# A causal attention block on one core: queries and keys projected for one unit at a time, fixed steps for each kind of piece, and a refilled opening and closing

## The chip, the cores and the metric

The kernel runs on one core of a Trainium2 chip. A core has five engines that work side by side, each with its own queue of instructions: TensorE (PE in the profile; its weight loads are listed apart as PEld), VectorE (DVE), ScalarE (ACT), GpSimd (POOL), and SyncE (SP), which in this kernel issues nearly all transfers (DMAs). Engines wait for one another through semaphores. The metric is the device time of one execution in microseconds (us); lower is better. All numbers are float32.

## The reference

The input x has 8 batches of 1024 tokens of 256 numbers. The block is a sandwich: half a routed feed-forward, attention, half a routed feed-forward, each added to x.

```python
x = x + 0.5 * ffn(layernorm(x), gate_w, w1, b1, w2, b2)
x = x + attention(layernorm(x), Wq, bq, Wkv, bkv, Wo, bo)
x = x + 0.5 * ffn(layernorm(x), gate_w, w1, b1, w2, b2)

# attention: 16 heads of 16 numbers, causal
dots = einsum('bhid,bhjd->bhij', q * scale, k)
attn = softmax(where(j > i, -1e9, dots))
out  = einsum('bhij,bhjd->bhid', attn, v) @ Wo.T + bo

# ffn: softmax gate over 8 experts, the two best of each token
counts = bincount(a_e, length=8)
keep   = counts <= cap            # an expert with more than cap tokens is dropped whole
```

With 8192 tokens, two experts each and 8 experts, cap is 1280 while the mean count is 2048, so an expert is kept only if it is chosen far less than the mean.

## The kernel before

**Two parts, of which one runs.** The kernel computes attention on x at once and, beside it, counts for both feed-forwards how many tokens choose each expert (`choose` L334, `tally`, `fewest` L397). Only if some expert has at most cap tokens does a branch (L1309) run the feed-forward and, where needed, the attention again. With these inputs no branch is taken, so the time is that of one call of `attention` (L681). The gate of the first feed-forward comes out of extra columns of the value projection, that of the second out of extra columns of the output projection; that is why both are 256 + 8 = 264 wide.

**Units and steps.** A unit u is four heads g of one batch b (u = 4b + g), 32 units in all, and one more, u = -1, in which only the first half of the work below exists for unit 0. Each unit has 24 steps. In a step PE computes two kinds of score blocks, each as matmuls on 32 by 64 tiles of the array: `sc` for the exponentials of unit u (`e_steps` L911: ACT exponentiates the block into `pT`, POOL masks a diagonal block by a select, PE later multiplies `pT` by the values into `pav`), and `sm` for the row maxima of unit u+1 (`m_steps` L865: DVE takes a maximum over each block; `settle` L899 sends the maxima by DMA into a row of `qT`, so that the next pass subtracts them inside its matmul). The widths of a step's blocks follow the causal mask: 512 in steps 0 and 1, 384 in 2 and 3, 256 in 4 and 5, 128 in 6 and 7, 512 in 8 to 17, 384 in 18 and 19, 256 in 20 and 21, 128 in 22 and 23. There are six score buffers of one PSUM bank each, taken in turn (`score` L695), and two banks for everything else (`bank` L699). Attention values of a step are issued two and three steps after its scores; steps 0, 2, 8 and 10 have none.

**Pieces beside the steps.** All other PE work is cut into pieces and put one (or half of one) into a step. `pq` is a projection of 512 tokens to queries or keys (eight matmuls of 512, in two half-steps); ACT adds the bias, and eight DMAs carry each head of 16 rows to its place in `qT` or `kT`. `pv` is the values of 128 tokens, `px` the output projection of 128 tokens (both eight matmuls of 264, in two half-steps), `pta` four transposes of the normalised input. Class `Beside` (L52) hands them out: each work is a Python generator that yields PIECE (wants to begin a piece), REST (the second half, at the next step) or a number of steps to wait. `Beside.step(begin)` lets the first work in its list that asks for a PIECE have one, if `begin` is true. Steps 4 to 7 and 20 to 23, where DVE has most to do for each step, begin none unless two works ask at once (L1288).

**What runs beside which unit.** `prepare` (L727) loads the next batch and takes its statistics on DVE; `enter` (L750) normalises on POOL, four tiles ahead (`bufs=4`, L759), and transposes in g = 1; `values_of` (L776) follows in g = 2 and 3; `residual` (L807) adds the output bias to x on POOL; `project` (L825) stands in g = 0 and in g = 2, each time for two units (u+2 and u+3): weights of keys and of queries are kept apart (`wkT`, `wqT`), a column group of 128 holds eight heads of one kind, and there are four pieces (keys and queries for each half of the tokens), three steps apart. `leave` (L987) reads the attention of one half of a batch back from DRAM, takes reciprocals of the row sums, multiplies (two POOL multiplications, L1012, two steps apart), and then gives four px pieces; it begins at step 9 of g = 3 for the first half and at step 2 of the next batch's g = 0 for the second. `gate_first` (L817) and `regate` (L1114) are the chains of small DVE operations of the gates. Statistics of the output rows are put in `light` (L1029), and one is taken per step.

**Order.** `InOrder` (L27) chains every instruction of PE, DVE, ACT and POOL in the order in which the Python code issues it, so a waiting instruction holds all behind it on its engine. Since this helper records them, nearly every line of the profile says L37; groups are told apart by the names of their tiles. SP's DMAs go in program order too.

**Opening and closing.** Before unit -1 the first batch is normalised and `project(0, ...)` makes keys and queries for units 0 and 1, half by half (L1174 to L1182); the DMAs of the second unit's heads go out behind each half (L861). In unit -1 run the turning of the value weights and the first half of the values (L1186), and in unit 0 the rest of the weights' work (`turning`: wos, then `gcs`, `pt_gc`, `pg`, `pb_v`, L255 to L290), the other values, `gate_first(0)` and the projection for units 2 and 3. In the last unit no maxima are left; `divided`, `leave_first` and `leave_last` (L1038 to L1111) take the attention of the last four heads straight from PSUM, transposing it (`pt_last`), dividing, transposing back (`on_last`) and projecting (`px_last`). After the last step what is left in `beside` is finished (L1292), then the first gate's count (L1294), then the second half's `leave_last` and `regate`.

Of the kernel before, what the change touches and what calls it, by code (L numbers as in the profile page):

```python
# [10 lines left out]
F32 = mybir.dt.float32  # L11
# [37 lines left out]
PIECE, REST = "piece", "rest"  # L49


class Beside:  # L52
# [10 lines left out]
    def advance(self, work):  # L63
        ask = next(work[0], None)
        if ask is None:
            self.works.remove(work)
        else:
            work[1] = ask if ask in (PIECE, REST) else self.now + ask
        self.open = work if ask == REST else None if self.open is work else self.open

    def due(self):
        for work in list(self.works):
            while work in self.works and work[1] not in (PIECE, REST) and work[1] <= self.now:
                self.advance(work)
# [4 lines left out]
    def step(self, begin):  # L79
# [4 lines left out]
        elif begin:  # L84
            for work in self.works:
                if work[1] == PIECE:
                    self.advance(work)
                    break
# [12 lines left out]
def macaron_kernel(  # L101
# [98 lines left out]
    wqT = const.tile([P, DC, D], F32, name="wqT")  # L200
    wkT = const.tile([P, DC, D], F32, name="wkT")
# [5 lines left out]
    bqT = const.tile([P, DC], F32, name="bqT")  # L207
    bkT = const.tile([P, DC], F32, name="bkT")
# [6 lines left out]
    def weights(pool, bank, matmul, transpose):  # L215
# [6 lines left out]
        with nc.allow_non_contiguous_dma(reason="two vectors of 256"):  # L222
            for src, dst in ((bkv[:D], bkT), (bq, bqT)):
                nc.scalar.dma_start(out=dst, in_=src.rearrange("(c p) -> p c", p=P))
# [6 lines left out]
        with nc.allow_non_contiguous_dma(reason="two vectors of 256"):  # L231
            nc.sync.dma_start(out=boT, in_=bo.rearrange("(c p) -> p c", p=P))
            nc.sync.dma_start(out=bvT, in_=bkv[D:].rearrange("(c p) -> p c", p=P))

        gpsimd.tensor_scalar(bqT, bqT, QSCALE, None, ALU.mult)

        def turn(wsb, dst):
# [4 lines left out]
            scalar.copy(dst, pt.rearrange("p (c d) -> p c d", c=DC))  # L242

        turn(wks, wkT)
        yield PIECE
        turn(wqs, wqT)
# [9 lines left out]
        yield PIECE  # L256
# [4 lines left out]
        vector.tensor_scalar(gcs, gsb, mean, None, ALU.subtract)  # L261
        pt = bank("pt_gc")
# [4 lines left out]
        bo_cols = const.tile([P, DC, P], F32, name="bo_cols")  # L267
        gpsimd.tensor_copy(bo_cols, boT.unsqueeze(2).to_broadcast([P, DC, P]))
        bv_cols = const.tile([P, DC, P], F32, name="bv_cols")
        gpsimd.tensor_copy(bv_cols, bvT.unsqueeze(2).to_broadcast([P, DC, P]))  # L270
# [363 lines left out]
    def feed_forward(layer, logits, src, dst):  # L634
        stack = ExitStack()
        with stack:
# [15 lines left out]
            for b in range(B):  # L652
# [5 lines left out]
                for j in range(TB):  # L658
                    xn = norm.tile([P, D], F32, tag="xn", name=f"xn_n{layer}_{b}_{j}", bufs=4)
# [21 lines left out]
    def attention(run_no, src, dst, gate0, logits, tally):  # L681
# [3 lines left out]
        with stack:  # L685
# [64 lines left out]
            def enter(b):  # L750
# [3 lines left out]
                xns = {}  # L754

                def normed(jj):
                    xns[jj] = []
                    for j in (2 * jj, 2 * jj + 1):
                        xn = norm.tile([P, D], F32, tag="xn", name=f"xn_a{b}_{j}", bufs=4)  # L759
                        gpsimd.tensor_scalar(  # L760
                            xn, xb[:, j, :D], mv[:, j, 0:1], rstd[:, j : j + 1], ALU.subtract, ALU.mult
                        )
                        xns[jj].append(xn)

                normed(0)
                normed(1)
                yield 3
                for jj in range(TB // 2):
                    yield PIECE
                    turned(b, jj, xns.pop(jj))  # L770
                    if jj + 2 < TB // 2:
                        normed(jj + 2)
# [52 lines left out]
            def project(u, apart, parts=(0, 512)):  # L825
                b, g = divmod(u, NG)
                xnT = xnTs[b]
                gp = g // 2
                for s0 in parts:
                    others = []  # L830
                    for wT, bT, dsts, scale in ((wkT, bkT, kTs, 1.0), (wqT, bqT, qTs, QSCALE)):
                        yield PIECE
                        pq = bank(f"pq{u}_{s0}")
                        for c in range(DC):
                            matmul_cols(
                                pq,
                                wT[:, c, gp * P : (gp + 1) * P],
                                xnT[:, c, s0 : s0 + 512],
                                start=(c == 0),
                                stop=(c == DC - 1),  # L840
                            )
                            if c + 1 < DC:
                                yield REST
                        packed = ap.tile([P, 512], F32, tag="packed", name=f"packed{u}_{s0}", bufs=4)
                        scalar.activation(packed, pq, AF.Identity, bias=bT[:, gp : gp + 1], scale=scale)
                        for k in range(8):
                            r = 32 * (k % 4)
                            to = dsts[(u + k // 4) % 4][r : r + HD, s0 : s0 + 512]
                            head = packed[HD * k : HD * (k + 1), :]
                            if apart and dsts is qTs and k % 4 == 0 and u > 2:  # L850

                                nc.sync.dma_start(
                                    out=dsts[(u + k // 4) % 4][HD::32, s0 : s0 + 512], in_=zeros
                                )
                            if apart or k < 4:
# [503 lines left out]
```

## Time and profile before

| | us |
|---|---|
| median of three runs | 1393.98 (1392.86 to 1394.01) |
| the profiled execution | 1393.18 |
| its span, first to last instruction | 1391.50 |
| of it before unit -1 | 24.15 |
| unit -1 | 29.36 |
| unit 0 | 57.09 |
| units 1 to 30 | 1226.30 |
| unit 31 and the closing | 54.60 |

The profile is a hardware record of one execution. Its page gives the busy time of each engine, the chain of work that ended last, and groups of instructions with their mean durations in ns and the idle time of their engine just before them. Stretches of the span can be asked for by themselves, with the busy time and number of instructions of each engine; so can the instructions one by one, as a timeline with start, duration, engine, operation, the tile written and the tiles read, a repeat count, and in square brackets the idle time before and what ended it. The granted clock of TensorE is 0.983 over the span, 1.00 in units 1 to 30, 0.83 in unit -1, 0.85 in unit 0, and 0.81 in the last stretch. Over units 1 to 30 PE is busy for 1223.39 us, DVE for 942.70, ACT for 726.82 and POOL for 365.01.

### The profile page before, as it was taken

Reading aid. Unit: us, or ns where it says so; the run is one execution under the profiler, and the core shown is the slowest. Engines: PE = TensorE matmul, PEld = TensorE weight load, DVE = VectorE, ACT = ScalarE, POOL = GpSimd, SP = SyncE. Lnnn points to the kernel's source line nnn. Section 1 sums busy time; section 2 is a strip of 40 time slices with the busy share of each in tenths; the row PEclk is TensorE's granted clock in tenths of the full one; section 3 lists DMA queues with packets and bytes.
Section 4 is the critical chain, followed back from the end, with each engine's and each line's share of the span. In section 5 each row is a group of like instructions: output and inputs, shape, how many; then the busy total and the mean of one; then the engine's idle time right before and its main releaser. Section 6 shows DMA issues by size and latency. Waiting matters only on the chain.

```text
span 1391.5 us, 51072 instructions
## 1 busy us (share of the span) xinstructions
PE 1352.3 (97%) x20664; PEld 456.6 (33%) x20664; DVE 1029.7 (74%) x3417; ACT 788.0 (57%) x1790; POOL 399.0 (29%) x720
## 2 busy tenths in 40 slices
PE   6999999999999999999999999999999999999994
PEld 2333333333333333333333333333333333323331
DVE  4757677876878868777778777787687786778854
ACT  3246655565655656555655656555665565655561
POOL 3015114241143412352131421424114331222221
PEclk9889999999999999999999999999999999999997
DMA  4010111212112210212112121122112111122100
GB/s 149 10 41 27 42 27 50 60 60 77 35 56 61 73 47 30 79 51 72 41 36 71 45 88 34 48 66 73 53 33 60 57 47 44 44 66 65 43 27 33
DMA packets 67021, 73.70 MB, mean 53 GB/s; under 512 B 24688, under 2 KB 42232, under 8 KB 66776
## 3 DMA queue, kind: packets, MB, share of 16 engines
q1 hardware_dynamic: 65688, 69.82, 16.5%
q8 instruction: 164, 2.69, 0.8%
q14 instruction: 81, 0.66, 0.2%
q10 hardware_dynamic: 1088, 0.53, 0.1%
HBM read 26.87 MB, written 26.20 MB: 38 GB/s over the span
## 4 chain that ended last, share of the span: by engine, by line
PE 91%; DVE 4%; POOL 2%; issue 1%; SPq 1%; DMA 1%; ACT 0%; ACTq 0%; DVEq 0%; POOLq 0%
PE sc L37 40%; PE pav L37 23%; PE sm L37 9%; PE pq L37 8%; PE pv L37 4%; PE px L37 4%; PE pta L37 1%; DVE sm L37 1%; POOL rstd_a L37 1%; POOL xa L37 1%; DVE first L37 0%; DMA bqT<-in_L_attn_bq_dram 0%; SPq L862 0%; POOL pT L37 0%; SPq L856 0%
## 5 line engine op out<-in xcount | busy, mean ns | idle before, releaser
L37 ACT ACTIVATE pT<-sc 128x512 f32<-128x512 f32 (+3 forms) x1536 | 668.9, 489 | 515.2 <-PE sm L37 395.5
L37 PE MATMUL sm<-kT,qT 32*64 32x512 f32 (+3 forms) x6144 | 759.8, 511 | 1.5 <-DMA qT<-packed 0.4
L37 PE MATMUL sc<-qT,kT 32*64 32x512 f32 (+3 forms) x6144 | 709.2, 508 | 0.0
L37 POOL TENSOR_SCALAR_AFFINE_SELECT pT<-pT 128x256 f32<-128x256 f32 x512 | 208.1, 410 | 927.6 <-ACT pT L37 926.5
L37 DVE TENSOR_REDUCE first<-sm 128x1 f32<-128x512 f32 x512 | 328.2, 684 | 141.9 <-PE sm L37 136.2
L37 PE MATMUL pav<-pT,vaug 128*32 128x256 f32 (+2 forms) x5120 | 386.7, 370 | 3.9 <-POOL pT L37 3.9
L37 DVE CUSTOM_DVE_ANT_0 sm<-sm,causal,first 128x256 f32<-128x256 f32 (+3 forms) x512 | 261.2, 556 | 76.5 <-PE sm L37 67.2
L37 PEld LDWEIGHTS sc<-qT,kT 32*64 32x64 f32 x6144 | 188.5, 130 | 355.5 <-ACT pT L37 256.3
L37 DVE CUSTOM_DVE_ANT_0 sm<-sm,causal 128x256 f32<-128x256 f32 (+3 forms) x512 | 241.6, 515 | 79.0 <-PE sm L37 74.2
L37 PEld LDWEIGHTS pav<-pT,vaug 128*32 128x32 f32 x5120 | 104.0, 108 | 367.8 <-issue 289.6
L37 PEld LDWEIGHTS sm<-kT,qT 32*64 32x64 f32 x6144 | 213.9, 130 | 29.7 <-DVE top L37 14.4
L37 DVE DVE_READ_ACCUMULATOR2_ANT top<- 128x1 f32 x1024 | 145.0, 142 | 0.0
L37 PE MATMUL pv<-wvT,xnT 128*32 128x264 f32 x1024 | 83.7, 400 | 0.0
L37 PE MATMUL px<-woT,on 128*32 128x264 f32 x960 | 76.1, 389 | 0.0
L37 PE MATMUL pq<-xnT,wkT 128*32 128x512 f32 x512 | 68.0, 607 | 1.4 <-ACT xnT L37 1.4
L37 POOL TENSOR_SCALAR xn_a<-xa,mv_a,rstd_a 128x256 f32<-128x256 f32 x56 | 67.9, 1223 | 1.2 <-PE pta L37 1.0
L37 PE MATMUL pq<-xnT,wqT 128*32 128x512 f32 x512 | 66.8, 596 | 0.0
L37 POOL TENSOR_TENSOR on<-on,inv 128x512 f32<-128x512 f32 (+1 forms) x32 | 40.9, 1278 | 12.5 <-DMA inv<-inv_d 12.5
L37 PEld LDWEIGHTS pv<-wvT,xnT 128*32 128x32 f32 x1024 | 29.0, 111 | 43.6 <-issue 26.2
L37 POOL TENSOR_TENSOR xa<-xa,bo_all 128x528 f32<-128x528 f32 x32 | 42.0, 1311 | 0.6
L37 ACT COPY vaug<-pv 128x256 f32<-128x256 f32 x64 | 24.4, 381 | 26.6 <-PE pv L37 26.6
L37 PEld LDWEIGHTS px<-woT,on 128*32 128x32 f32 x960 | 27.9, 109 | 35.1 <-issue 11.4
(126 smaller groups left out, 482.2 us busy)
## 6 DMA issues: line engine op xcount, KB each, us to landing
att_d<-att SPq DMA_DIRECT2D x62, 256.0 KB
kT<-packed SPq DMA_DIRECT2D x256, 32.0 KB
qT<-packed SPq DMA_DIRECT2D x256, 32.0 KB
out_dram<-xa SPq DMA_DIRECT2D x16, 512.0 KB
on<-att_d SPq DMA_DIRECT2D x30, 256.0 KB
inv<-inv_d SPq DMA_DIRECT2D x30, 256.0 KB
xa<-in_L_attn_x_dram SPq DMA_DIRECT2D x7, 1024.0 KB
xa<-in_L_attn_x_dram SPq DMA_DIRECT2D x2, 512.0 KB
```

The costliest lines, as they stand in the source:

```text
L37: i = call(*args, **kwargs)
```

## The change

The weights of keys and queries are laid side by side in `wkqT`, the scale of the queries multiplied in when the weights are turned, so that one piece of 128 columns makes keys and queries of one unit (four heads each). `project(u)` has two pieces, one for each half of the tokens, and every unit but the last two runs one for unit u+2, as its first work. Its pieces are of a kind of their own (QK): they begin at step 0 or 8, and px, pv and pta pieces at the other steps. In `leave` the waits are shortened and the two multiplications follow one another, at the first step of a unit. `enter` normalises all eight tiles ahead (`bufs=8`) and its transposes follow. In the opening, `project(0)` is for unit 0 alone, `project(1)` is cut up into unit -1, which now takes two half-steps of pieces in each pair of steps, and `gcs` and the copies of the bias are computed three steps ahead of `pt_gc`. At the end, `leave_last` of the second half is interleaved with the rest of `regate` of the first half and with the first gate's count, and these with one another. The functions keep their arithmetic.

```diff
-PIECE, REST = "piece", "rest"
+PIECE, QK, REST = "piece", "qk", "rest"
...
-    def step(self, begin):
+    def step(self, kinds=()):
         self.now += 1
         self.due()
         if self.open is not None:
             self.advance(self.open)
-        elif begin:
+            return
+        for kind in kinds:
             for work in self.works:
-                if work[1] == PIECE:
+                if work[1] == kind:
                     self.advance(work)
-                    break
+                    return
...
-        turn(wks, wkT)
+        turn(wks, wkqT[:, :, :, 0, :], 1.0)
         yield PIECE
-        turn(wqs, wqT)
+        turn(wqs, wkqT[:, :, :, 1, :], QSCALE)
...
         turn(wos, woT[:, :, :D])
-        yield PIECE
...
         vector.tensor_scalar(gcs, gsb, mean, None, ALU.subtract)
+        bo_cols = const.tile([P, DC, P], F32, name="bo_cols")
+        gpsimd.tensor_copy(bo_cols, boT.unsqueeze(2).to_broadcast([P, DC, P]))
...
+        yield 2
+        yield PIECE
         pt = bank("pt_gc")
...
-                normed(0)
-                normed(1)
-                yield 3
+                for j in range(TB):
+                    xn = norm.tile([P, D], F32, tag="xn", name=f"xn_a{b}_{j}", bufs=8)
...
+                    if j % 2:
+                        yield 2
                 for jj in range(TB // 2):
                     yield PIECE
-                    turned(b, jj, xns.pop(jj))
-                    if jj + 2 < TB // 2:
-                        normed(jj + 2)
+                    turned(b, jj, xns[2 * jj : 2 * jj + 2])
...
-            def project(u, apart, parts=(0, 512)):
+            def project(u, parts=(0, 512)):
...
                 for s0 in parts:
-                    others = []
-                    for wT, bT, dsts, scale in ((wkT, bkT, kTs, 1.0), (wqT, bqT, qTs, QSCALE)):
-                        yield PIECE
...
+                    yield QK
+                    pq = bank(f"pq{u}_{s0}")
+                    for c in range(DC):
+                        matmul_cols(
+                            pq,
+                            wkqT[:, c, g].rearrange("p a d -> p (a d)"),
...
+                        if c + 1 < DC:
+                            yield REST
...
+                    for k in range(8):
+                        r = 32 * (k % 4)
+                        nc.sync.dma_start(
+                            out=(kTs, qTs)[k // 4][u % 4][r : r + HD, s0 : s0 + 512],
+                            in_=packed[HD * k : HD * (k + 1), :],
+                        )
...
             def leave(b, hf):
...
-                yield 2
+                waits = (2, 6, 5, 9) if hf else (2, 4, 4, 5)
+                yield waits[0]
...
-                yield 6
+                yield waits[1]
                 vector.reciprocal(sums, sums)
...
-                yield 4
+                yield waits[2]
...
-                yield 8
+                yield waits[3]
                 for c in range(DC):
                     gpsimd.tensor_tensor(on[:, c], on[:, c], inv[:, c], ALU.mult)
-                    yield 2
+                yield 2
...
-                drain(project(0, 0, (hf * 512,)))
+                drain(project(0, (hf * 512,)))
...
-            opening = beside.add(chain(some(turning, 2), values_of(0, 0, 0, HT)))
+            opening = beside.add(chain(some(turning, 2), project(1), values_of(0, 0, 0, HT)))
...
                 if u == 0:
                     beside.finish(opening)
+                    preparing = beside.add(prepare(1))
+                    opening = beside.add(values_of(0, 0, HT, TB), first=True)
+                    projecting = beside.add(project(2))
                     beside.add(chain((PIECE,), turning, residual(0), gate_first(0)))
...
+                    valuing = beside.add(values_of(b + 1, 0, 0, HT))
+                if u >= 0 and g == 3 and b + 1 < B:
+                    beside.finish(valuing)
+                    valuing = beside.add(chain(values_of(b + 1, 0, HT, TB), residual(b + 1)))
+                if u > 0:
+                    beside.finish(projecting)
+                    if u + 2 < NU:
+                        projecting = beside.add(project(u + 2), first=True)
...
-                    beside.step(True)
+                    for _ in range(2):
+                        beside.step((QK, PIECE))
...
-                    beside.step(k in long_steps or u == 0 or beside.pending() > 1)
+                    if u == 0:
+                        beside.step((PIECE, QK))
+                    elif k in (0, 8):
+                        beside.step((QK, PIECE))
+                    else:
+                        beside.step((PIECE,) if k in long_steps or beside.pending() > 1 else ())
...
-            while beside.works:
-                beside.finish(beside.works[0])
-            leasts = [None if gate0 is None else fewest("0", gate0[1], bank("cnt0"))]
-            drain(leave_last(B - 1, 1, last.pop(), (scalar.copy, vector.tensor_copy)))
+            while beside.open is not None or beside.pending():
+                beside.step((PIECE,))
+            leasts = [None]
+            for k, _ in enumerate(leave_last(B - 1, 1, last.pop(), (scalar.copy, vector.tensor_copy))):
+                for _ in range(3 if k < 2 else len(beside.works) * STEPS):
+                    beside.step()
+                if k == 1 and gate0 is not None:
+                    leasts = [fewest("0", gate0[1], bank("cnt0"))]
```

## The prediction, made before the changed kernel had run

> **What bounds the kernel now.** I read the page's busy shares and chain of waits first, then the busy time of each engine in chosen stretches, then the timeline of TensorE (PE) step by step, and last the built order of both kernels on each engine, which says in which step each instruction stands. The page:
>
> ```profile
> span 1391.5 us, 51072 instructions
> PE 1352.3 (97%) x20664; PEld 456.6 (33%) x20664; DVE 1029.7 (74%) x3417; ACT 788.0 (57%) x1790; POOL 399.0 (29%) x720
> PE 91%; DVE 4%; POOL 2%; issue 1%; SPq 1%; DMA 1%; ACT 0%; ACTq 0%; DVEq 0%; POOLq 0%
> ```
>
> PE is the path: 97% busy, 91% of the chain. So what counts is how long PE's steps are, and a busy PE is not a full one. The stretches (unit -1, unit 0, the four units of one inner batch, the last unit; columns: length, busy of PE, PEld, DVE, ACT, POOL, clock, DMA):
>
> ```profile
> 23.40:53.50 30.10, 29.58 (x270) 9.13 (x262) 23.80 (x76) 4.62 (x9) 0.00 (x0) 0.83 0.12 29
> 53.50:110.60 57.10, 53.81 (x691) 18.49 (x689) 33.89 (x115) 26.62 (x61) 12.30 (x24) 0.85 0.10 26
> 724.80:767.28 42.48, 42.48 (x658) 13.22 (x657) 32.83 (x111) 24.47 (x55) 11.72 (x22) 1.00 0.22 61
> 767.28:807.72 40.44, 40.31 (x645) 14.51 (x641) 31.68 (x103) 24.30 (x56) 19.93 (x28) 1.00 0.18 60
> 807.72:850.69 42.97, 42.97 (x677) 13.84 (x673) 30.29 (x103) 25.67 (x59) 6.58 (x16) 1.00 0.22 61
> 850.69:889.50 38.81, 38.49 (x612) 13.52 (x608) 31.64 (x105) 23.09 (x55) 11.49 (x22) 1.00 0.12 39
> ```
>
> See two things: units of one batch are uneven (42, 40, 43, 39 us, 164.5 together), and unit 0 takes 57 us at clock 0.85. A step is measured from the first score matmul of one to that of the next:
>
> ```profile
> 744.88 0.65 PE L37 MATMUL sc<-qT,kT 32*64 32x512 f32 x2
> ...
> 747.35 0.65 PE L37 MATMUL sc<-qT,kT 32*64 32x512 f32 x2
> ...
> 749.83 0.64 PE L37 MATMUL sc<-qT,kT 32*64 32x512 f32 x2
> ...
> 751.88 0.65 PE L37 MATMUL sc<-qT,kT 32*64 32x512 f32 x2
> ```
>
> A 512-wide step with half a projection piece (pq) in it takes 2.47 us (744.88 to 747.35), with half an output piece (px) 2.05. Read so, the steps repeat to 0.01 us from unit to unit. Where unit 0 loses:
>
> ```profile
> 90.47 0.59 PE L37 MATMUL sc<-qT,kT 32*64 32x512 f32 x2
> ...
> 94.14 0.26 PE L37 MATMUL pt_gc<-ident,gcs 8*128 8x8 f32 x2 [2.47 <-DVE gcs L37]
> ...
> 94.97 1.07 PE L37 MATMUL sc<-qT,kT 32*64 32x512 f32 x2
> ```
>
> PE stands idle 2.47 us for `gcs`, and the same matmul then takes 1.07 instead of 0.59 us, until 104.
>
> [...] half a px piece costs 0.45 us in a step that already has attention values (pav, same tiling; 2.06 against 1.61) and 0.72 in a step without (1.63 against 0.91). [...]
>
> **The change, part by part.**
>
> *Work.* Instruction counts on every engine are equal in both built orders (a projection of one unit has k and q of four heads in 128 columns, where one of two units had two times 128). Nothing is removed; the sum changes only by where things stand.
>
> *Projection and pieces in inner units.* Before, units g=0 and g=2 hold four pq pieces, g=1 and g=3 none; after, each unit holds two, at steps 0/1 and 8/9, and its px or values (pv) pieces at 2/3, 10/11, 12/13, 14/15; g=1 has its four transposes (pta) at 16 to 19. Medians of the same steps before: 0 to 3: 2.04+2.26+1.41+2.04 = 7.75; 4 to 7: 1.19+1.15+0.98+0.97 = 4.29; 8 to 11: 2.04+2.26+1.63+2.32 = 8.25; 12 to 15: 4x2.06 = 8.24; 16 to 19, empty: 1.61+2.01+1.40+1.67 = 6.69; 20 to 23: 4.48. Sum 39.7. With transposes 16 to 19 is 2.20+2.20 and two 384-wide ones, not seen, taken as 1.99 (2.20 less the 0.21 by which a px step is shorter at 384; bounds 1.85 and 2.3): 41.4. A batch is 3x39.7+41.4 = 160.5 against 164.5: a pq piece costs 1.00 us at 8/9 (4.30 against 3.30 empty) and 1.4 at 12 to 17 (4.94 against 3.5 to 3.6).
>
> *What is late next: DVE.* The freed time was DVE's. In g=0 `gate_first` puts 22 small operations of some 0.21 us into steps 9 to 16. DVE's work in steps 11 to 16 (two reductions of 0.63 a step, px addition 0.43, statistics 0.53, gate operations) is 14.3 us after; the same steps of PE were 14.1 us before, and are 2.32+4x2.06+1.61 = 12.2 after. PE needs DVE's first reduction of a step for the score buffer of the next, so the lack shows: followed step by step it comes to 2.0 us. g=1 has the other gate chain at 18 to 23 and into g=2: 5.2 us of DVE work in steps 20 to 23 of 4.5: 0.9. In g=3 POOL's `rstd` (1.67 us) and residual additions (1.31 each) stand among selects, as before (cost then 1.1): 0.6, since they start two steps earlier. Together 3.5 a batch: 164.0, so -0.5 a batch. The bounds: no new stall (as many as before, 1.8 a batch) gives -2.2; twice mine gives +3. Units 2 to 29 are seven batches: -3.5; unit 1 gets two pq pieces that it had not (+1), units 2 and 3 lack the gate chain's worst (-1.5). I take -4 for all inner units.
>
> *DMAs.* SP carries the same issues. After, eight (4 k, 4 q; 0.62 us each, 5 us) follow each pq piece. In the built order the row that step 8 needs stands ahead of the first eight, and the sums of `leave` behind the second: issued about 11 us after step 8, landed some 2 us later (inv took 3.5 us from issue to use at 1311.5), while the reciprocal stands at step 15, 16.8 us after. Covered by 3 us.
>
> *Rows divided at a first step.* Both multiplications (1.28 us each) now stand behind the select of step 0, ahead of that of step 1. That exponential ends 4.3 us into the unit, the select is done at 5.6, and PE wants it in step 3 at 6.8. Cost 0; what is queued behind is the select, then pav; slack 1.1 us.
>
> *Unit -1.* Before, the first k and q of two units are projected ahead, and SP issues the second unit's heads before the first unit's second half: DVE waits at 33 to 42 us, 4.5 us in sum. After, the second half lands by 29 us. The first start stays (eight issues of 0.6 us behind the 17.45 packing, as now, end at 22.4). But two projections of eight now stand in the 384- and 256-wide steps, where PE gets about 1.8 us more each, and DVE idles about 2.5 us. -1.5 (bounds -3.5, +3 if PE's clock is low there).
>
> *Unit 0.* Steps 0 to 7 keep 16.3 us. The rest was 40.8: 20.2 for 8 to 15, 4.34+5.39+4.59 for `pt_gc`, `pg`, `pb_v`, and 6.3. After: transposes of wos 1.85 (0.91+0.65+0.27 switch), pq 2.26+2.04, pt_gc 2.1 (1.61+0.26+switch; `gcs` is computed three steps ahead), pg 3.2 (twelve records at 0.125, half of what the low clock took), pb_v 2.9 (1.07 likewise), pq 4.94, then 3.62+3.07+4.48 = 30.5, and 0.9 for the gate chain that now begins here. 31.4 against 40.8: -9.4 (bounds -12, -5 if the clock stays low).
>
> *Closing.* The last unit's transposes waited for the other half's gate chain:
>
> ```profile
> 1365.73 0.37 ACT L37 COPY att_last<-pav 128x256 f32<-128x256 f32 x1 [1.25 <-PE pav L37]
> ...
> 1368.48 1.14 PE L37 MATMUL pt_last<-ident,att_last 128*128 128x128 f32 x4 [2.83 <-DVE counts L37]
> ```
>
> After, DVE's copy stands ahead of 18 of these operations, so pt_last starts at 1365.8; eight stand ahead of the division, the rest ahead of the copy of `on`, and px_last begins at about 1370.1 instead of 1371.86. -1.8 (bounds -3, 0).
>
> Sum: -4 -1.5 -9.4 -1.8 = -16.7. The profiled execution took 1393.18 us with 1391.5 of span, 0.8 us under the median of 1393.98; the span becomes 1374.8, the median 1377.3.
>
> **Rivals.** (1) No new DVE stalls, as the small operations slip into gaps: -15 in the inner units in place of -4, 1366 us. For it: DVE is busy only 74%; against: one queue in order, and 14.3 us do not fit into 12.2. (2) The opening doesn't pay: unit -1 costs 3 us more with PE at low clock (0.83 there now), unit 0 gains 5: 1386. (3) Slower: the two multiplications meet a late POOL. From 1.1 us of lag every further us holds pav in each of 14 halves; the full 2.56 us less nothing is at most 36 us, a likely 2 us each 28: 1405. For it: POOL has `rstd` and residual additions just ahead in g=3; against: 11 us of work in the 13 us before. (4) Nothing moves, as DVE takes it all: 1393.
>
> **How the numbers follow.** Main case 0.62 (own range 1371 to 1384), rival 1 0.17, 2 0.11, 3 0.06, 4 0.04. The range 1366 to 1388 holds the main case and most of 1 and 2. A difference under 0.2% (2.8 us) can't be told from none here: faster 0.89, same 0.04, slower 0.07.
>
> **What would show it.** Right: unit 0 near 48 us without the idle before `pt_gc`; inner units 40 to 42 us with pq steps of 2.04 and 2.26; steps 14 to 18 of g=0 longer than 2.06 and 1.61 with PE waiting for DVE; pt_last 2.5 us after pav no more. Wrong: PE waiting for POOL at step 3 of g=0 and g=1, or g=0 under 40 us.

## The result and the profile after

The changed kernel takes 1375.99 us (median of four runs, 1375.38 to 1377.18), the kernel before, run beside it, 1393.78 (1392.86 to 1394.01): a ratio of 0.9875, 95% interval 0.9857 to 0.9892. The forecast was 1377.3. The profiled execution took 1375.38 us with a span of 1373.6. Its page:

```profile
span 1373.6 us, 51244 instructions
PE 1336.6 (97%) x20664; PEld 445.5 (32%) x20664; DVE 1038.2 (76%) x3417; ACT 785.5 (57%) x1790; POOL 398.1 (29%) x720
PE 95%; DVE 3%; DMA 1%; issue 1%; POOL 0%; ACT 0%; SPq 0%; ACTq 0%; POOLq 0%
```

The instructions per engine are the same (PE 20664, DVE 3417, ACT 1790, POOL 720). PE still sets the end, with 95% of the chain instead of 91%: the 2% of it that were POOL's are gone. The stretches that answer to those shown of before (unit -1, unit 0, the four units of one inner batch, the last unit; length, busy of PE, PEld, DVE, ACT, POOL, clock, DMA):

```profile
23.10:53.60 30.50, 30.20 (x294) 10.81 (x294) 24.12 (x76) 4.96 (x10) 0.00 (x0) 0.80 0.14 31
53.60:99.93 46.33, 46.33 (x659) 16.92 (x655) 34.40 (x119) 25.27 (x60) 14.32 (x26) 0.95 0.08 21
708.96:750.14 41.18, 41.18 (x644) 13.15 (x640) 33.70 (x116) 23.09 (x54) 9.83 (x20) 1.00 0.21 63
750.14:792.59 42.45, 42.07 (x660) 14.25 (x657) 32.76 (x106) 25.46 (x58) 20.84 (x29) 1.00 0.23 72
792.59:832.34 39.75, 39.75 (x644) 13.03 (x641) 29.59 (x97) 24.30 (x56) 6.21 (x16) 1.00 0.14 37
832.34:872.23 39.89, 39.89 (x644) 13.11 (x640) 31.53 (x104) 24.32 (x57) 12.81 (x23) 1.00 0.19 52
1319.90:1373.60 53.70, 31.71 (x456) 12.80 (x452) 22.35 (x93) 21.24 (x54) 10.97 (x24) 0.83 0.10 34
```

Unit 0 went from 57.1 to 46.3 us at clock 0.95 instead of 0.85, which is more than half of the gain. The batch is 163.27 us instead of 164.74 (in the other inner batches 163.0 to 163.8 instead of 163.3 to 164.5). Taken from the starts of the units in the two profiled executions:

| part | before | after | difference | forecast |
|---|---|---|---|---|
| up to the end of unit -1 | 53.51 | 53.60 | +0.09 | -1.5 |
| unit 0 | 57.07 | 46.33 | -10.75 | -9.4 |
| units 1 to 30 | 1226.3 | 1220.0 | -6.33 | -4 |
| unit 31 and closing | 54.56 | 53.66 | -0.90 | -1.8 |
| span | 1391.46 | 1373.56 | -17.9 | -16.7 |

Within the inner units the steps came out as forecast almost everywhere: the projection takes 2.04 and 2.26 at steps 0 and 1 and again at 8 and 9, pieces at 12 to 15 take 2.06 each, and two transposes in 384-wide steps take 1.99 each, the number that had been worked out for an unseen case. What remains is where the step sums were left by a wait, and the opening and closing. Those are what the runs below are about. An inner step repeats from run to run to 0.02 us; the span does not repeat so well, because of the opening and of what follows the last count. So what a run below changes in the inner units is read from the lengths of units and steps.

### The profile page after: what moved, and what is told of

Read it like the earlier page. It is cut to its first block, busy times and chain, and to the rows that moved or that the text cites. A ratio compares the mean times of both kernels' runs of the same rounds, so it can differ in the third digit from the quotient of the medians.

```text
span 1373.6 us, 51244 instructions
## 1 busy us (share of the span) xinstructions
PE 1336.6 (97%) x20664; PEld 445.5 (32%) x20664; DVE 1038.2 (76%) x3417; ACT 785.5 (57%) x1790; POOL 398.1 (29%) x720
## 4 chain that ended last, share of the span: by engine, by line
PE 95%; DVE 3%; DMA 1%; issue 1%; POOL 0%; ACT 0%; SPq 0%; ACTq 0%; POOLq 0%
PE sc L37 42%; PE pav L37 24%; PE sm L37 10%; PE pq L37 9%; PE pv L37 5%; PE px L37 4%; PE pta L37 1%; DVE sm L37 1%; DMA bkqT<-in_L_attn_bq_dram 0%; DVE cand_g L37 0%; SPq L846 0%; PE px_last L37 0%; DVE top L37 0%; DVE first_g L37 0%; DVE oh_g L37 0%
## 5 line engine op out<-in xcount | busy, mean ns | idle before, releaser
L37 PE MATMUL sc<-qT,kT 32*64 32x512 f32 (+3 forms) x6144 | 693.8, 507 | 0.0
L37 PE MATMUL pav<-pT,vaug 128*32 128x256 f32 (+2 forms) x5120 | 381.8, 370 | 2.2 <-POOL pT L37 1.5
L37 PEld LDWEIGHTS sc<-qT,kT 32*64 32x64 f32 x6144 | 183.1, 130 | 345.9 <-ACT pT L37 266.8
L37 PEld LDWEIGHTS sm<-kT,qT 32*64 32x64 f32 x6144 | 210.8, 130 | 33.4 <-DVE top L37 21.5
L37 PE MATMUL pq<-xnT,wkqT 128*32 128x512 f32 x1024 | 136.5, 608 | 1.3 <-ACT xnT L37 1.3
L37 ACT ACTIVATE packed<-pq,bkqT 128x512 f32<-128x512 f32 x64 | 45.4, 710 | 11.7 <-PE pq L37 11.7
L37 POOL TENSOR_TENSOR on<-on,inv 128x512 f32<-128x512 f32 (+1 forms) x32 | 40.3, 1282 | 14.1 <-DMA inv<-inv_d 14.1
L37 PEld LDWEIGHTS pq<-xnT,wkqT 128*32 128x32 f32 x1024 | 25.9, 110 | 55.5 <-issue 52.0
```

What stands on the lines that cost most here:

```text
L37: i = call(*args, **kwargs)
```

## The experiments

Each run is the changed kernel with the edit shown. Unit numbers are those of the batch 16 to 19 where no other is given; "now" in an expectation is the changed kernel.

**1. The first gate's chain, moved to another unit.**

```diff
-                    if g == 0 and b and k == 9:
+                    if g == 2 and b and k == 9:
                         beside.add(gate_first(b))
```

> The changed kernel with one line altered: the chain of the first gate's small DVE operations begins at step 9 of g=2 instead of step 9 of g=0 (batches 1 to 7). My theory (14.3 us of DVE work in steps 11 to 16 against 12.2 of PE): steps 14 to 18 of g=0, now 2.40, 2.06, 1.64, 2.54, 2.06, fall to 2.06, 2.06, 1.61, 2.0, 1.40, so g=0 goes from 41.2 to 39.7 us; g=2 has no statistics and no output additions in those steps, DVE's work there with the chain is about 12 us against 12.2, so g=2 stays within 0.3 of 39.75. Seven batches: the span falls by 8 to 11 us. Rival (the stretch in g=0 comes from the output additions or from POOL, not from the gate chain): g=0 stays at 41.2 and g=2 gains the chain's price, span the same or up to 5 us longer.

g=0 fell from 41.18 to 39.89 us in every batch, g=2 rose from 39.75 to 40.00; steps 14, 17 and 18 of g=0 went from 2.40, 2.54 and 2.06 to 2.06, 2.01 and 1.66. Net 1.05 us a batch; units 1 to 30 took 7.0 us less, although g=2 of the last batch rose by 0.75 (the span, 1363.1, fell by more because of its opening, see run 7). The timeline of DVE of the changed kernel, up to the first reduction of step 17 (start, duration, engine, line, operation, tiles, idle before):

```profile
738.42 0.19 DVE L37 TENSOR_SCALAR cand_f<-cand_f 128x64 f32<-128x64 f32 x1
738.64 0.23 DVE L37 TENSOR_TENSOR cand_f<-cand_f,iota_e 128x64 f32<-128x64 f32 x1
738.90 0.22 DVE L37 TENSOR_REDUCE first_f<-cand_f 128x8 f32<-128x64 f32 x1
739.15 0.22 DVE L37 TENSOR_TENSOR oh_f<-cand_f,first_f 128x64 f32<-128x64 f32 x1
739.30 0.42 DVE L37 TENSOR_TENSOR xa<-px,xa 128x264 f32<-128x264 f32 x1
739.64 0.75 DVE L37 CUSTOM_DVE_ANT_0 sm<-sm,causal,first 128x512 f32<-128x512 f32 x1
```

and the timeline of PE of the same kernel in step 17:

```profile
739.53 0.65 PE L37 MATMUL sc<-qT,kT 32*64 32x512 f32 x2
739.55 0.65 PE L37 MATMUL sm<-kT,qT 32*64 32x512 f32 x2
739.72 0.88 PE L37 MATMUL sc<-qT,kT 32*64 32x512 f32 x4
740.03 0.59 PE L37 MATMUL sm<-kT,qT 32*64 32x512 f32 x2
740.20 0.59 PE L37 MATMUL sc<-qT,kT 32*64 32x512 f32 x2
740.50 1.07 PE L37 MATMUL sm<-kT,qT 32*64 32x512 f32 x4
```

In step 15 of the same unit the eight pairs of score matmuls start within 0.52 us of one another (735.83 to 736.35); here the last one starts 0.97 us after the first. DVE has no idle time, it is still at four operations of the chain and an output addition while PE needs its score buffers back. PE is shown as busy all the time, and the wait stands in no idle column: it is to be read from the distance of the starts. That the small operations cause it is shown by moving them, since PE's own work in those steps stayed the same.

**2. The second gate's chain, thirteen steps later.**

```diff
-            def regate(b, j0, j1):
+            def regate(b, j0, j1, wait=3):
...
-                yield 3
+                yield wait
...
-                        beside.add(chain(leave(b - 1, 1), regate(b - 1, 0, TB)))
+                        beside.add(chain(leave(b - 1, 1), regate(b - 1, 0, TB, 16)))
```

> The changed kernel with the second gate's chain started 13 steps later: regate waits 16 steps instead of 3 after the last output piece, so that its operations fall into steps 7 to 16 of g=2 instead of steps 18 of g=1 to 1 of g=2. Theory (DVE is the stall in steps 20 to 23 of g=1): steps 22 and 23 of g=1 go from 1.65 and 1.41 to 1.1 and 0.97, step 0 of g=2 from 2.23 to 2.04; g=1 from 42.4 to 41.4, g=2 unchanged at 39.6 to 40.0. Seven batches: span down by 6 to 9 us. Rival (the price only moves with the chain): g=2 gains what g=1 loses, span the same.

g=1 fell from 42.45 to 41.33 and g=2 from 39.75 to 39.56; steps 22 and 23 of g=1 from 1.65 and 1.41 to 0.98 and 0.97. In the last batch g=2 (unit 30) rose by 1.01; there four output additions (1.6 us) stand on DVE in the same steps. The theory holds, 1.31 us a batch and 8.6 us over units 1 to 30: here the chain is free in a unit in which DVE has time for it. The two runs together give the stalls of a batch: 1.30 and 1.31 us are the two chains.

**3. The small centred gate matrix, computed late again.**

```diff
+        yield 2
+        yield PIECE
         mean = const.tile([E, 1], F32, name="g_mean")
...
         vector.tensor_scalar(gcs, gsb, mean, None, ALU.subtract)
-        yield 2
-        yield PIECE
         pt = bank("pt_gc")
```

> The changed kernel with the four DVE operations that make gcs put back right ahead of pt_gc, in step 11 of unit 0 (the piece itself stays there). Theory (PE idles for gcs and then runs at a low clock): an idle of 2 to 2.5 us ahead of pt_gc, then score matmuls of 1.07 instead of 0.59 to 0.65 us for some 6 us; unit 0 longer by 4 to 8 us (46.3 to 50 to 54). Rival A (only the wait counts): longer by 2.0 to 2.5 us, no low clock. Rival B (the gain of unit 0 came from the pieces' places alone): under 1 us.

Unit 0 took 49.33 instead of 46.33 us: step 11 3.67 instead of 1.83, step 12 4.61 instead of 3.11, and step 10 0.3 less. The timeline of PE there:

```profile
75.05 0.64 PE L37 MATMUL pav<-pT,vaug 128*32 128x256 f32 x8
77.49 0.26 PE L37 MATMUL pt_gc<-ident,gcs 8*128 8x8 f32 x2 [1.80 <-DVE gcs L37]
77.67 1.12 PE L37 MATMUL sc<-qT,kT 32*64 32x512 f32 x2
...
78.58 1.06 PE L37 MATMUL sc<-qT,kT 32*64 32x512 f32 x2
```

and of the changed kernel:

```profile
76.76 0.64 PE L37 MATMUL pav<-pT,vaug 128*32 128x256 f32 x8
77.33 0.28 PE L37 MATMUL pt_gc<-ident,gcs 8*128 8x8 f32 x2
77.55 0.65 PE L37 MATMUL sc<-qT,kT 32*64 32x512 f32 x2
...
78.03 0.59 PE L37 MATMUL sc<-qT,kT 32*64 32x512 f32 x2
```

An idle of 1.80 us is followed by score matmuls of 1.12 and 1.06 us instead of 0.65 and 0.59. So half of the price of the wait, 1.5 of 3.0 us, falls on the step behind it. The kind is as the theory had it, the size is under its 4 to 8 us, because the wait was shorter and the low clock ended at 81.12, within step 12 (2.70 in step 13, as without the wait). Of the 10.75 us of unit 0 some 3 are this part of the change, with the pieces where they now stand. In the kernel before, the low clock behind its wait of 2.47 us lasted from 94.64 to 104.88, three times as long as in this run, and the three steps of `pt_gc`, `pg` and `pb_v` took 14.32 us instead of 7.64. So an estimate from the two profiles is 6.7 us for the wait and the low clock, 3.4 for the places of the other pieces and 0.7 for steps 0 to 7; this division was not tried alone.

**4. and 5. More work on POOL ahead of the divisions.** Two more multiplications with a result that nothing reads, and one more:

```diff
                 yield waits[3]
+                spare = ap.tile([P, DC, 512], F32, tag="spare", name=f"spare{b}_{hf}", bufs=1)
+                for c in range(DC):
+                    gpsimd.tensor_tensor(spare[:, c], inv[:, c], inv[:, c], ALU.mult)
                 for c in range(DC):
```

> The changed kernel with two more POOL multiplications of the same shape (1.28 us each, result unused) ahead of the two that divide the rows, at the first step of g=0 and g=1. Theory (the select behind them has 1.1 us of slack before PE wants it in step 3): 2.56 us more on POOL show as about 1.5 us in step 3 of g=0 and of g=1 (2.04 to about 3.5) in each of batches 1 to 7: span longer by 15 to 22 us. Rival 1 (more slack than that): step 3 stays at 2.04 and nothing moves. Rival 2 (no slack): 2.56 in each, 36 us.

> The changed kernel with one more POOL multiplication (1.28 us, unused) ahead of the two at the first step of g=0 and g=1. Two more cost 0.85 to 0.93 us a unit, so the slack is 2.56 less 0.9, about 1.7 us, if it is a threshold. Theory (threshold): one more, 1.28 us, is free: step 2 of g=0 and g=1 stays at 1.41, units within 0.1, and only opening and closing differ. Rival (every us on POOL costs a third of a us): 0.4 more in each, step 2 about 1.8.

With two, g=0 and g=1 took 0.85 and 0.93 us more, in step 2 (2.31 and 2.37 instead of 1.41); with one, none of units 1 to 30 moved by more than 0.02. Units 1 to 30 took 12.5 us more with two, where 15 to 22 had been expected, and 0.2 with one. It is a threshold, and the rival of a third of a microsecond for each falls. POOL and PE with two more:

```profile
717.33 2.04 POOL L37 TENSOR_TENSOR spare<-inv 128x512 f32<-128x512 f32 x2
719.33 2.50 POOL L37 TENSOR_TENSOR on<-on,inv 128x512 f32<-128x512 f32 x2
721.78 0.41 POOL L37 TENSOR_SCALAR_AFFINE_SELECT pT<-pT 128x256 f32<-128x256 f32 x1
```

```profile
720.65 0.65 PE L37 MATMUL px<-woT,on 128*32 128x264 f32 x8 [0.82 <-POOL on L37]
721.23 0.54 PE L37 MATMUL sc<-qT,kT 32*64 32x384 f32 x2
```

What waits is not the attention values of step 3 behind the select, but the output piece in step 2, which needs the first multiplication itself. The spare ones took 2.04 us for the two (1.04 each) and not 2.56, so the slack is 2.04 less 0.82, 1.2 us, and not 1.7 as the second expectation had it; one spare multiplication is just under it.

**6. The second projection at steps 12 and 13.**

```diff
-                    elif k in (0, 8):
+                    elif k in (0, 12):
```

> The changed kernel with the second projection of a unit at steps 12 and 13 instead of 8 and 9; the output and value pieces move up to 8 to 11. Theory (a piece's price depends on the steps it stands in, read off before: steps 8 and 9 with an output or value piece 1.63+2.12 instead of 2.04+2.26, steps 12 and 13 with the projection 2.47+2.47 instead of 2.06+2.06): g=2 and g=3 longer by 0.27 us each (39.75 to 40.0, 39.9 to 40.2), g=1 likewise; g=0 shorter or the same, since the longer steps give DVE 0.8 us before the gate chain stalls it (41.2 to between 40.5 and 41.3). Span up by 3 to 7 us. Rival (pieces cost the same wherever they stand): every unit the same within 0.1, except g=0.

g=1, g=2 and g=3 took 0.28 us more in nearly every batch, where 0.27 was worked out; the steps are 1.63, 2.12 and 2.47, 2.47, as read off before. Units 1 to 30 took 7.8 us more. The rival, that a piece costs the same everywhere, falls. g=0 took 0.18 more, where less or no more was expected: with shorter steps 8 to 11 DVE is behind already in step 12 (2.92 instead of 2.47), and only part of that comes back later.

**7. Matmuls that keep PE busy while it waits for the first heads.** Their result is not read.

```diff
+            warm = bank("warm")
+            for _ in range(3):
+                matmul_cols(warm, ident, xnTs[0][:, 0, :512])
             for kT in kTs[2:]:
```

> The changed kernel with 24 more matmuls of a 32-column weight and 512 columns (a result that nothing reads) at the point where PE waits for the first heads, 21.8 to 23.1 us. Theory (unit -1 missed its forecast because PE runs at half clock from 23 to 31 us and DVE lacks maxima): the first steps of unit -1, now 5.25, 4.06 and 2.47, fall to about 4.3, 3.3 and 2.4 at clock near 1.0, unit -1 ends 1.5 to 2.5 us earlier. Rival (the transfers of the heads set those steps): the same to within 0.3, or later by up to 0.5 for the matmuls added.

The first two pairs of steps of unit -1 took 2.64 and 2.68 instead of 5.25 and 4.06 (the first started 0.8 us later), and unit -1 ended at 50.41 instead of 53.60, more than the theory had it. But the other runs, run 11 apart, have the same opening as the changed kernel, and in them it ended anywhere between 50.35 and 53.78. The stretch from 24 to 30 us, of the changed kernel, of run 2 and of run 1:

```profile
24.00:30.00 6.00, 5.74 (x40) 2.18 (x42) 2.83 (x9) 1.20 (x3) 0.00 (x0) 0.54 0.22 50
```

```profile
24.00:30.00 6.00, 5.74 (x44) 2.15 (x46) 3.90 (x13) 1.59 (x3) 0.00 (x0) 0.72 0.23 52
```

```profile
24.00:30.00 6.00, 5.95 (x70) 2.22 (x74) 4.92 (x17) 1.44 (x4) 0.00 (x0) 1.00 0.21 48
```

At clocks 0.54, 0.72 and 1.00 DVE got 2.83, 3.90 and 4.92 us of work, and unit -1 ended at 53.60, 52.26 and 50.35. The same opening is granted a different clock in this stretch from run to run. So this single run does not show that the matmuls brought the clock: run 1 had it without them.

**8. The closing as before.**

```diff
-            while beside.open is not None or beside.pending():
-                beside.step((PIECE,))
...
+            while beside.works:
+                beside.finish(beside.works[0])
+            leasts = [None if gate0 is None else fewest("0", gate0[1], bank("cnt0"))]
+            drain(leave_last(B - 1, 1, last.pop(), (scalar.copy, vector.tensor_copy)))
```

> The changed kernel with the closing of the kernel before: what is left of the first half's gate is finished first, then the first count, then the last heads' leave. Theory: everything up to the last step is the same, and the closing is longer by what the last stretch gained, 0.9 us (unit 31 from 53.7 to 54.6); pt_last waits for DVE's counts again. Rival (the 0.9 came from elsewhere in unit 31): the same within 0.2.

The timeline of PE in this run's closing:

```profile
1350.31 1.14 PE L37 MATMUL pt_last<-ident,att_last 128*128 128x128 f32 x4 [2.82 <-DVE counts L37]
1352.15 1.09 PE L37 MATMUL on_last<-ident,normed 128*128 128x128 f32 x4 [0.70 <-DVE normed L37]
1353.69 3.77 PE L37 MATMUL px_last<-woT,on 128*32 128x264 f32 x32 [0.46 <-ACT on L37]
```

and in that of the changed kernel:

```profile
1349.05 0.90 PE L37 MATMUL pt_last<-ident,att_last 128*128 128x128 f32 x4 [0.50 <-ACT att_last L37]
...
1352.07 0.87 PE L37 MATMUL on_last<-ident,normed 128*128 128x128 f32 x4 [1.95 <-DVE cand_g L37]
1353.40 3.31 PE L37 MATMUL px_last<-woT,on 128*32 128x264 f32 x32 [0.46 <-DVE least L37]
```

The wait for `counts` is back, 2.82 us (2.83 before). Counted from the start of the last two steps, the last projection began after 9.82 us here (9.83 in the kernel before) and after 8.11 in the changed kernel; the last count after 21.36 (21.36) and 19.63. The closing's part of the change is thus -1.7 us; in the other runs that have the new closing the last count came 1.5 to 2.3 us earlier than in the kernel before. Unit 31 with the closing took 54.89 us here, 1.2 more than in the changed kernel, where 0.9 was expected; the rival, that nothing changes, falls. What comes from the last count to the end took 7.6 to 8.9 us in the runs with no order to it, and in the profiled execution of the changed kernel it was 0.6 more than before; unit 31 ahead of its last step took 0.2 more. That is why the table above shows only -0.9.

**9. The waits of `leave` as before.**

```diff
-                waits = (2, 6, 5, 9) if hf else (2, 4, 4, 5)
+                waits = (2, 6, 4, 8)
...
                     gpsimd.tensor_tensor(on[:, c], on[:, c], inv[:, c], ALU.mult)
-                yield 2
+                    yield 2
```

> The changed kernel with the waits of leave as in the kernel before (2, 6, 4, 8 steps, the two multiplications two steps apart): they fall into steps 6 to 9 of g=0 for the first half, and its four output pieces stand at steps 10 to 17 of g=0 instead of 2, 3 and 10 to 15. Nothing else moves. Theory (steps are added up: 2 and 3 empty cost 3.0 instead of 3.45, 16 and 17 with a piece 4.1 instead of 3.6 without a stall, and DVE's work up to step 17 is the same): g=0 the same within 0.5 (41.2), span within 4 us: the early division gained nothing by itself. Rival (the early place of the first piece is what makes g=0 short): g=0 longer by 1 us or more, span by 7 or more.

g=0 took 0.43 us less in each batch: steps 2 and 3 were 0.71 and 2.30 instead of 1.41 and 2.04 (0.44 less), and steps 16 to 18 with the piece 2.47, 2.16 and 1.61 instead of 1.64, 2.54 and 2.06 (the same sum). The theory holds. The early place of the first division costs 3.0 us over units 1 to 30 and gains nothing.

**10. No piece begun at step 14.**

```diff
-  beside.step((PIECE,) if k in long_steps or beside.pending() > 1 else ())
+  beside.step((PIECE,) if k in long_steps and (k != 14 or g == 1) or beside.pending() > 1 else ())
```

> The changed kernel with no piece begun at step 14 of g=0, g=2 and g=3: the fourth piece stands in 15 and 16, and the empty steps are 14 and 17 to 19 instead of 16 to 19. In g=2 steps 16 to 19 are 1.61, 2.01, 1.40, 1.67 now: the second of two empty 512-wide steps is 0.40 longer than the first. Theory (a single empty step is cheap, the second one in a row meets DVE's and ACT's reading of the score buffers): step 14 is 1.61, 15 and 16 are 2.06, 17 is 1.61: g=2 and g=3 shorter by 0.3 to 0.5 each, span down by 4 to 7 us. Rival (the 0.40 belongs to the steps themselves, to their selects and maxima): nothing moves, within 1 us.

The theory falls. Step 14 was 1.61 and step 17 1.61 instead of 2.01, but step 15, now behind a single empty step, took 2.33 instead of 2.06, and step 18 1.80 instead of 1.40: the 0.40 moved, and g=2 grew by 0.27. g=0 fell by 0.45, since its steps 14 to 23 added up to less; why was not traced. g=3 grew by 1.02, for a reason that the theory had not considered, and units 1 to 30 took 5.0 us more. POOL there:

```profile
871.97 1.67 POOL L37 TENSOR_TENSOR rstd_a<-ve_a,half 128x8 f32<-128x8 f32 x1
873.72 0.21 POOL L37 TENSOR_TENSOR std<-ve_a,rstd_a 128x8 f32<-128x8 f32 x1
873.88 0.77 POOL L37 TENSOR_SCALAR_AFFINE_SELECT pT<-pT 128x256 f32<-128x256 f32 x2
```

and PE:

```profile
873.35 0.52 PE L37 MATMUL pav<-pT,vaug 128*32 128x192 f32 x4
874.34 0.52 PE L37 MATMUL pav<-pT,vaug 128*32 128x192 f32 x4 [0.47 <-POOL pT L37]
```

The residual additions begin when the last value piece is done. One step later, `rstd` meets the selects of the short steps, and step 21 takes 2.06 us instead of 1.08.

**11. and 12. The parts together, with and without spare matmuls.** The first gate's chain begins at step 0 of g=2 (in the last batch it stays in g=0), the second's as in run 2; run 11 also has the matmuls of run 7, and two groups of them in each of the last four pairs of steps of unit -1.

```diff
-                    if g == 0 and b and k == 9:
+                    if b and (g, k) == ((0, 9) if b + 1 == B else (2, 0)):
```

> The changed kernel with three alterations together: the first gate's chain begins at step 0 of g=2 (in the last batch it stays at step 9 of g=0), the second gate's chain 13 steps later in steps 8 to 16 of g=2, and spare matmuls on PE while it waits for the first heads and in the last four steps of unit -1. Theory (the parts add up: 1.3 less 0.2 us in six batches, 1.3 in seven less 1.0 in the last, opening at full clock 2 to 4): g=0 39.9, g=1 41.3, g=2 39.6 to 40.0, and the span falls by 15 to 21 us from 1373.6, to 1353 to 1359. Rival (both chains in one unit are too much for DVE there): g=2 longer by 1.5 to 3 us, the span only 5 to 10 us down.

> The same as the run with the three alterations, without the spare matmuls. Theory (the granted clock in the first steps of unit -1 and at its end is left to chance without them): the times lie 1 to 4 us above those with spare matmuls, and scatter more, while every inner unit is the same to 0.05 us. Rival (the spare matmuls do nothing or only delay the first step): the same median within 1 us.

With spare matmuls 1365.61 us (five runs, 1362.95 to 1366.23), ratio to before 0.9803, interval 0.9784 to 0.9823; without, 1366.11 (1364.70 to 1367.68), ratio 0.9812, interval 0.9792 to 0.9832. Both intervals lie below the changed kernel's. The gain over the changed kernel is 10 us and not 15 to 21: g=0 and g=1 came to 39.89 and 41.31 as expected, but g=2 rose to 40.75, with step 4 to 8 at 1.37, 1.45, 1.13, 1.09 and 2.44 instead of 1.19, 1.15, 0.97, 0.97 and 2.04. The rival was nearer there. The first gate's operations stand in just these short steps now; that they are in the way there, even though DVE has less to do in that unit, is read from their place and was not tried alone. So the two gains do not add: units 1 to 30 took 1210.8 us in run 12, 1211.4 with the second chain's move alone (run 2) and 1212.9 with the first's (run 1).

The spare matmuls bring 0.5 us in the medians, which the scatter covers, where 1 to 4 were expected: the rival of run 12 holds. In the profiled execution PE stood at clock 1.00 up to the closing, and unit 0 took 43.72 us instead of the 46.24 of run 12; but the spare matmuls in the end of unit -1 stretched its ninth pair of steps from 2.47 to 4.72 us, and unit -1 ended at 53.28. Whether those of run 7 alone hold the clock in every run was not tried with repeated runs.

## Why the prediction was right

The forecast of the likeliest case, 1377.3, is 1.3 us off. Part of this closeness is luck: by the table the terms missed by +1.6 (unit -1), -1.4 (unit 0), -2.3 (inner units) and +0.9 us (closing), which nearly cancel, and the opening alone ends up to 3.4 us apart from run to run. What was right is the mechanism of most terms. By its steps:

- **Inner units.** The additive reading of steps held: 160.5 us for a batch without stalls was forecast, and three units of 39.56 and one of 41.31, the shortest that the runs show without and with transposes, make 159.99 (g=0 itself came to no less than 39.88; its last 0.3 us were not traced). The stalls were put at 3.5 us (g=0 2.0, g=1 0.9, g=3 0.6) and came to 3.28: 1.62 in g=0, 1.14 in g=1, 0.19 in g=2 and 0.33 in g=3. Runs 1 and 2 show that 1.30 of g=0, 1.12 of g=1 and 0.19 of g=2 are the gate chains on DVE, as the step had it (with its chain gone g=1 took 41.33, where 41.4 was worked out for no stall), and that refutes the first rival, in which they slip into gaps. Both terms were a little high, which makes -1.2 us a batch instead of -0.5, and with unit 1's +1.07 (forecast +1) and a unit 30 for which there was no term (+0.86) the inner units gave -6.3 instead of -4.
- **g=3.** The 0.6 was laid to POOL. What is there, 0.33, is gone in unit 27, which is also a g=3 but has no further batch to prepare (39.56); the preparation has statistics on DVE and `rstd` on POOL, and which of them it is was not separated. That POOL can cost there is shown by run 10, one step later.
- **Unit 0.** -9.4 forecast, -10.75 measured. Steps 8 to 23 were put at 31.4 us and took 30.73; transposes, `pt_gc`, `pg` and `pb_v` were put at 1.85, 2.1, 3.2 and 2.9 and took 1.63, 1.83, 3.11 and 2.70. The 0.27 for a switch in the first two was an estimate, the 0.72 less the 0.45 us that half an output piece costs in a step without and with attention values; where the 0.27 goes was not shown. Against these, the projection in steps 9 and 10 was put at 4.30 and took 4.89, and of the 0.9 for the gate chain at most 0.5 is seen. The other 0.7 us is in steps 0 to 7, which had been left as they were and ran at clock 0.50 for 5.1 us (53.60 to 58.67) instead of 6.8 (53.68 to 60.51). Run 3 shows the mechanism, idle time that is paid twice.
- **Unit -1.** This is the term that was wrong: -1.5 forecast, +0.09 in the profile. DVE was to idle about 2.5 us between the projections; it idled 4.9 (1.46, 1.46, 0.99, 0.62 and 0.41 between the maxima), while PE was granted a clock of 0.50 for 6.8 us (24.53 to 31.36). In run 1, with the same opening at clock 1.00, the idle times are 0.58, 0.30, 0.62 and 0.41, together 1.9, and unit -1 ended 3.2 us earlier than in the kernel before; so the size of the term hangs on the clock, as the prediction's bounds (-3.5 and +3) allowed for. From the timeline of DVE in the changed kernel:

```profile
26.47 0.70 DVE L37 CUSTOM_DVE_ANT_0 sm<-sm,causal 128x512 f32<-128x512 f32 x1 [1.46 <-PE sm L37]
...
29.99 0.57 DVE L37 CUSTOM_DVE_ANT_0 sm<-sm,causal 128x384 f32<-128x384 f32 x1 [1.46 <-PE sm L37]
...
33.15 0.43 DVE L37 CUSTOM_DVE_ANT_0 sm<-sm,causal 128x256 f32<-128x256 f32 x1 [0.99 <-PE sm L37]
```

  The first maxima did not stay where they were, as the step had it, but began 1.0 us earlier (23.14), which hid part of this. The runs with the same opening lie between -3.2 and +0.3.
- **Closing.** -1.8 forecast; -1.7 up to the last count, by run 8. The mechanism is that of the forecast.
- **Rows divided at a first step.** The cost was put at 0, with 1.1 us of slack for the select behind. Run 5 confirms that it was free of waits, and run 4 that the slack, 1.2, belongs to another instruction, the output piece in step 2; that the two numbers are near is chance. But the same edit moved a piece to a dearer place, and run 9 shows 0.43 us a batch for that. The sum for the inner units had the piece at its new place (1.41 and 2.04) and steps 16 and 17 empty, which by itself is about even; what it did not see is that emptying them saves nothing in g=0, where DVE is behind: steps 16 to 18 add up to the same 6.24 us in run 9. The third rival (slower by POOL) had its mechanism right and its point of decision nearly, but nothing ran late.
- **Transfers.** No wait of PE, DVE or POOL for a row or for the reciprocals appeared in units 1 to 29; the output pieces at step 2 took 1.41, as before. POOL's only waits for the reciprocals, 14.1 us in three, are in the last two units.

## What to carry to other kernels

Where one in-order engine is full, price a piece of work by the step it stands in, read from the same step elsewhere in the trace, and then follow the engine that frees the buffers step by step: both sums together gave a batch within 0.5%. A moved chain of small operations belongs into the unit whose steps leave that engine time, and not merely into the unit with the least of its work. An edit that moves a wait also moves everything that the wait held back, and that has a price of its own.

## What the hardware showed beyond that

- Right behind a 1.80 us idle of PE in run 3, score matmuls took 1.12 and 1.06 us instead of 0.65 and 0.59, at a granted clock of 0.50. Two stretches of run 3 (length, busy of PE, PEld, DVE, ACT, POOL, clock, DMA):

```profile
77.70:81.12 3.42, 3.42 (x28) 1.00 (x27) 1.37 (x3) 1.26 (x3) 0.00 (x0) 0.50 0.22 47
74.28:77.70 3.42, 1.62 (x30) 0.38 (x15) 2.75 (x8) 1.63 (x3) 0.00 (x0) 1.00 0.18 47
```

  The low clock lasted from 77.70 to 81.12. In the 3.42 us ahead of it the clock was 1.00 and PE was busy for 1.62.
- One and the same opening ended between 50.35 and 53.78 us, with the clock granted from 24 to 30 us (1.00 down to 0.50, in run 12). In the traces of the two kernels and of runs 1, 2 and 12 the times at which the clock changes lie whole multiples of 3.41 us apart, to 0.02 us (in the changed kernel 24.53, 31.36, 48.43 and 58.67), and these times differ from run to run: clock 0.50 from 24.53 to 31.36 in the changed kernel, from 26.34 to 29.75 in run 2, and nowhere from 16.79 to 47.51 in run 1. The place of these times is not all of it: run 12 has its changes where run 1 has them (47.52 and 47.51) and was at clock 0.50 from 23.63 to 30.45 all the same. The kernel before scattered likewise, 1388.15 to 1394.57 in eight runs, with a mean clock of 0.988 and 0.983 in the shortest and the longest.
- The clock also fell while PE was shown as busy. From 45.02 to 48.43 us of the changed kernel, in the end of unit -1, PE's records fill the whole 3.41 us, but with only 26 matmuls (54 from 38.20 to 41.60), and DVE is busy all the time; from 48.43 to 58.67 the clock is 0.50. In run 11, with spare matmuls in those steps, it stayed at 1.00.
- POOL multiplications of 128x512 took 1.04 us in runs 4 and 5, with one tile as both inputs and another as the result, and 1.27 to 1.30 with two different inputs, of which one was also the result. Which of the two differences it is was not tried.
